# A gated scan followed by a mixture of experts: wo products of each expert's third set and the join of its outputs moved, Gelu of c11 behind the third copy of z, transposes behind the fourth z product

## The chip, the core and the metric

The kernel runs on one core of a Trainium2 chip. The metric is the device time of a run in microseconds, lower is better. A run is one execution of the whole program; the profile is of one execution of its own, taken by the hardware profiler.

Engines are called as the profile calls them: PE (TensorE, matmul; PEld its weight loads), DVE (VectorE), ACT (ScalarE), POOL (GpSimd), SP (SyncE, which issues most of the DMAs).

## The reference, cut to what matters

```python
def reference(x, w_qkva, gamma, router_w, w0, w1, wo):      # x: 8 x 1024 x 256, all float32
    x = x + attn(layernorm(x), w_qkva, gamma)               # rmsnorm, projections, gated scan over the tokens
    return x + ffn(layernorm(x), router_w, w0, w1, wo)

def ffn(x, router_w, w0, w1, wo):                           # 8 groups of 1024 tokens, 8 experts
    logits = einsum('GSM,ME->GSE', x, router_w)
    dispatch, combine = gating_top2(logits, C=256)          # each expert takes up to 256 tokens of a group
    expert_inputs = einsum('GSEC,GSM->EGCM', dispatch, x)
    layer_w0 = einsum('EGCM,EMH->EGCH', expert_inputs, w0)  # M = 256, H = 1368
    layer_w1 = einsum('EGCM,EMH->EGCH', expert_inputs, w1)
    hidden = gelu(layer_w0) * layer_w1
    expert_outputs = einsum('EGCH,EHM->EGCM', hidden, wo)
    return einsum('EGCM,GSEC->GSM', expert_outputs, combine)
```

The change touches only the expert part: the three einsums with w0, w1 and wo.

## The kernel before

**Blocks, experts, sets.** The eight groups are taken in four blocks of two. In each block the eight experts follow each other; an expert has two groups of 256 gathered tokens, and its hidden width of 1368 is cut into six *sets*: five of 256 channels and a last one of 88. There are 4 x 8 x 6 = 192 sets, and `run_set` writes out the instructions of one. This part of the program is scheduled by hand: every engine runs its instructions in the order in which the Python code issues them (`tc.manual_schedule()`).

**The two hidden products with seven matmuls.** For a set, w0 and w1 against the two halves of the model dimension are the 2x2 blocks a11, a12, a21, a22; the tokens of the two groups are the 2x2 blocks b11, b12, b21, b22. Instead of eight block products the kernel uses the seven of a Strassen-Winograd scheme, with sums s1 to s4 of the weights (`row_sums`, on POOL) and t1 to t4 of the tokens (`column_sums`, on DVE). `st.mm` is one such product: one matmul of 128x128 by 256 for each of the set's two chunks of 128 channels. In the trace a float32 matmul leaves two records, so a full-width product shows as four records, all at line L701.

Four products accumulate one after the other in the PSUM bank `z`, and between them ACT copies the running sum out ("snapshots"), because each of them is needed:

- z = a11 b11, copied to `snap0` (L861); the bank `pa` gets a12 b21, and DVE adds both: `c11` (L867), to which ACT applies Gelu (L875 in the kernel before).
- z += s2 t2, copied to `snap1` (L874); the bank `pb` gets s1 t1.
- z += s3 t3, copied to `snap2` (L883); DVE adds it to `pb` and writes half of `hid` (L884).
- z += a22 t4; DVE multiplies z by c11 into the other half of `hid` (L890). The next set starts z anew.
- pb += s4 b22; DVE adds snap1 to it, which is `c12` (L826, `first_sum`). Its Gelu (L829, `first_gate`) and the product with the first half (L833, `second_gate`) are issued in the next set.

So a z product waits for the copy of the one before, and the next set's first z product waits for L890. What is issued on PE between two z products covers the copy.

**The wo products.** `hid` times `wo` of a set is again taken with seven products, with POOL's sums of wo (`out_sums`) and DVE's sums of `hid` (`hid_sums`: L764, then L767 and L768). They are issued two sets later. `out_work` lists them in the order p1, p2, p4, p7, p6, p5, p3 for a full set, or as p2, p3, p4 and x for the set of 88; `products(n)` issues the next n of the list between the z products. Each is one matmul (two records, L753) that accumulates over the six sets of an expert in half of one of four banks: p1 and p6 in y0, p2 and p3 in y1, p7 and p5 in y2, p4 and x in y3. There is one bank of each name, so the next expert's first products must wait until the last expert's sums have been read.

Because of the two sets of delay, an expert's last wo products (those of its sixth set) are issued in the *second* set of the next expert (`st.s == 1`), all four of them ahead of the second z product. In that set `join_outputs` combines the four banks into the output `yT`: part 0 copies half of y0 to `u` on ACT (L798) and adds the rest of y0 and part of y2 on DVE (L799, L800); part 1 adds y1 (L804), y2 (L805) and y3 (L809). The next expert's first wo products, p1 and p2 of its first set, come in its *third* set, behind the first z product.

The last two experts of the last block are `plain`: their wo product is done directly (`outputs`, L733), one set later, in four parts of two matmuls.

**What is put between.** `between()`, called once in a set, puts four 128x128 transposes into the bank `aside`: in the fourth and fifth set of an expert those of the next expert's gathered tokens (`px`, L627, copied by ACT at L630), in the third and sixth those of the last expert's output (`pt_y`, L818, copied by ACT at L717 and then stored by a DMA that SP issues). `pump()`, called twice in a set (behind the pb product in the middle, and at the end), issues the planned pieces of everything else: the scan part of the next block's tokens, its gating, and the sums of the block before. These use the one bank `aside` too.

The lines that the two kernels name alike are a few lines apart: the three copies of z are L861, L874, L883 before and L869, L881, L889 after; L867, L884, L890 and L826 are L875, L891, L898 and L827; Gelu of c11 is L875 before and L890 after. Where the text names a line without more, it is that of the kernel before.

Of the kernel before, what the change touches and what calls it, by code (L numbers as in the profile page):

```python
# [8 lines left out]
FP = mybir.dt.float32  # L9
I32 = mybir.dt.int32  # L10
BF = mybir.dt.bfloat16
AF = mybir.ActivationFunctionType
ALU = mybir.AluOpType
# [4 lines left out]
def kernel(  # L18
# [12 lines left out]
    P = 128  # L31
    B, N, D = x.shape
    NE, _, H = w0.shape
    KC = D // P
    G, S = B, N
    CAP = (int(2.0 * S / NE) + 3) // 4 * 4
# [9 lines left out]
    GB = 2  # L46
# [11 lines left out]
    pb = ctx.enter_context(tc.tile_pool(name="experts", bufs=2))  # L58
# [4 lines left out]
    def bank(tag, name):  # L63
        return psum.tile([P, 512], FP, tag=tag, name=name, bufs=1)
# [600 lines left out]
    def plain(n, e):  # L665
        return n == NB - 1 and e >= NE - 2
# [91 lines left out]
    def hid_sums(st, half):  # L758

        b11, b12, b21, b22 = [st.hid[:, g, k, :] for k in range(2) for g in range(2)]  # L760
        V = nc.vector
        if half == 0:
            st.tw = pb.tile([P, 4, CAP], FP, tag="tw", name=f"tw_{st.n}_{st.e}_{st.s}", bufs=2)
            V.tensor_tensor(st.tw[:, :2, :], st.hid[:, 1], st.hid[:, :, 0], ALU.subtract)  # L764
            return
        t1, t3, t2, t4 = (st.tw[:, i, :] for i in range(4))
        V.tensor_tensor(t2, b22, t1, ALU.subtract)  # L767
        V.tensor_tensor(t4, b21, t2, ALU.subtract)  # L768
        st.t = t1, t2, t3, t4

    def out_work(st):

        if plain(st.n, st.e):
            return [lambda q=q: outputs(st, q) for q in range(4)]
        if st.s == NS - 1:
            def one(name, g, i):
                hs = st.hs
                add_product(st, name, wos[st.j][:hs, 0, i * P : (i + 1) * P], st.hid[:hs, g, 0, :])
            return [lambda: one("p2", 0, 0), lambda: one("p3", 0, 1),
                    lambda: one("p4", 1, 0), lambda: one("x", 1, 1)]  # L780
        a11, a12, a22, s1, s2, s3, s4 = osums.pop(st.j)
        b11, b21, b22 = st.hid[:, 0, 0, :], st.hid[:, 0, 1, :], st.hid[:, 1, 1, :]
        t1, t2, t3, t4 = st.t
        return [lambda p=p: add_product(st, *p) for p in (
            ("p1", a11, b11), ("p2", a12, b21), ("p4", s4, b22), ("p7", s3, t3),
            ("p6", s2, t2), ("p5", s1, t1), ("p3", a22, t4),
        )]

    yts = {}

    def join_outputs(n, e, part):

        V = nc.vector
        acc = {k: ys[n, e, i] for k, (i, half) in ACC.items()}
        halves = [acc[k].rearrange("p (h s) -> p h s", h=2) for k in ("p1", "p2", "p7", "p4")]
        if part == 0:
            u = yts["u"] = pb.tile([P, 3, CAP], FP, tag="u", name=f"u_{n}_{e}", bufs=1)
            nc.scalar.copy(u[:, 0, :], halves[0][:, 0, :])  # L798
            V.tensor_tensor(u[:, 1, :], u[:, 0, :], halves[0][:, 1, :], ALU.add)  # L799
            V.tensor_tensor(u[:, 2, :], u[:, 1, :], halves[2][:, 0, :], ALU.add)  # L800
            return
        u = yts.pop("u")
        yt = pb.tile([P, 2, GB, CAP], FP, tag="yT", name=f"yT_{n}_{e}", bufs=1)
        V.tensor_tensor(yt[:, :, 0, :], u[:, 0::2, :], halves[1], ALU.add)  # L804
        V.tensor_tensor(  # L805
            yt[:, :, 1, :], u[:, 1:3, :],
            halves[2][:, 1:2, :].to_broadcast([P, 2, CAP]), ALU.add,
        )
        V.tensor_tensor(yt[:, :, 1, :], yt[:, :, 1, :], halves[3], ALU.add)  # L809
        for i in range(4):  # L810
            ys.pop((n, e, i))
        yts[n, e] = yt

    def output_rows(n, e, gl):
        pt = ps_a(f"pt_y{n}_{e}_{gl}")
        for hh in range(NH):
            for i in range(2):
                nc.tensor.transpose(  # L818
                    pt[:, hh * D + i * P : hh * D + (i + 1) * P],
                    yts[n, e][:, i, gl, hh * P : (hh + 1) * P], ident,  # L820
                )
        keep_output(n, e, gl, pt)

    def first_sum(st):
        st.c12 = st.ten("cg", "c12", 3)
        nc.vector.tensor_tensor(st.c12, st.snap1, st.cut(st.pb), ALU.add)  # L826

    def first_gate(st):
        nc.scalar.activation(st.c12, st.c12, AF.Gelu_apprx_tanh)  # L829

    def second_gate(st):
        h22 = st.h2[: st.hs, 1, st.wide]
        nc.vector.tensor_tensor(h22, h22, st.c12, ALU.mult)  # L833

    def run_set(j, last, due, pump, between):


        V, A = nc.vector, nc.scalar
        st = Set(j)
        a11, a12, a22, s1, s2, s3, s4 = st.a  # L840
        b11, b21, b22, t1, t2, t3, t4 = st.b
        nm = f"{st.n}_{st.e}_{st.s}"
        z, p_a, p_b = bank("z", f"z_{nm}"), bank("pa", f"pa_{nm}"), bank("pb", f"pb_{nm}")
        st.pb = p_b
        st.hid = pb.tile([P, GB, 2, CAP], FP, tag="hid", name=f"hid_{nm}", bufs=3)
        st.h2 = st.hid.rearrange("p g c s -> p g (c s)")
        zz = st.cut(z)
        work = [f for o in due for f in out_work(o)]
        summed = last and last.s < NS - 1 and not plain(last.n, last.e)
        joined = units[units.index((st.n, st.e)) - 1] if st.s == 1 and j > NS else None  # L850
        if joined and plain(*joined):
            joined = None

        def products(share):
            for _ in range(min(len(work), share)):
                work.pop(0)()

        more = 2 * (len(due) > 1)
        st.mm(z, a11, b11, True)
        snap0 = st.ten("snap", "sn0", 4)  # L860
        A.copy(snap0, zz)  # L861
        if last:
            first_gate(last)
        products(2 + more)
        st.mm(p_a, a12, b21, True)
        c11 = st.ten("cg", "c11", 3)
        V.tensor_tensor(c11, snap0, st.cut(p_a), ALU.add)  # L867
        if last:
            second_gate(last)  # L869
        if st.s == 1:  # L870
            products(2)
        st.mm(z, s2, t2, False)
        st.snap1 = st.ten("snap", "sn1", 4)
        A.copy(st.snap1, zz)  # L874
        A.activation(c11, c11, AF.Gelu_apprx_tanh)  # L875
        products(1 + more)
        if joined:
            join_outputs(*joined, 0)
        st.mm(p_b, s1, t1, True)
        pump()  # L880
        st.mm(z, s3, t3, False)  # L881
        snap2 = st.ten("snap", "sn2", 4)
        A.copy(snap2, zz)  # L883
        V.tensor_tensor(st.h2[: st.hs, 1, st.wide], snap2, st.cut(p_b), ALU.add)  # L884
        if summed:
            hid_sums(last, 0)
        products(2)
        between()
        st.mm(z, a22, t4, False)  # L889
        V.tensor_tensor(st.h2[: st.hs, 0, st.wide], zz, c11, ALU.mult)  # L890
        products(8)  # L891
        st.mm(p_b, s4, b22, False)
        first_sum(st)
        if summed:
            hid_sums(last, 1)
        if joined:
            join_outputs(*joined, 1)
        pump()  # L898
        return st

# [72 lines left out]
    with tc.manual_schedule():  # L973
        last, pending, late = None, [], [[] for _ in range(UB)]
        for n in range(NB):
# [22 lines left out]
            def pump():  # L998
                for f in plan.pop(at[0], []):
                    f()  # L1000
                j, half = at[0] // 2 + n * NE * NS, at[0] % 2
                e, s = at[0] // (2 * NS), j % NS
                nxt = (n, e + 1) if e + 1 < NE else (n + 1, 0)
                if nxt in units:
                    if half == 0 and s == 0 and e + 1 < NE:
                        gather_unit(*nxt)
                    if s == (4, 5)[1 - half]:
                        column_sums(*nxt, 1 - half)
                at[0] += 1

            def between():
                q = at[0] // 2
                e, s = q // NS, q % NS
                nxt = (n, e + 1) if e + 1 < NE else (n + 1, 0)
                if s in (3, 4) and nxt in units:
                    input_channels(*nxt, s - 3)
                before = (n, e - 1) if e > 0 else (n - 1, NE - 1)
                if s in (2, 5) and before in yts:
                    output_rows(*before, s // 5)
                    if s == 5:  # L1020
                        yts.pop(before)

            for j in range(n * NE * NS, (n + 1) * NE * NS):
# [4 lines left out]
                due = [o for o in pending if due_in(o) <= j]  # L1028
                pending = pending[len(due):]
                last = run_set(j, last, due, pump, between)  # L1030
# [41 lines left out]
```

## Time and profile before

| | us |
|---|---|
| median of 3 runs | 2142.76 (2138.98 to 2143.45) |
| the profiled execution, its own time | 2141.66 |
| its span in the profile | 2139.7 |
| first set to the start of the last one | 130.5 to 2111.7 |

The span is cut by the expert sets: they run from 130.5 us to the end, but for some 25 us. Before them come the loads and the first block's scan. In the table of groups a row reads: line, engine, operation, output <- inputs (buffer numbers left out), shape, count; busy time and mean of one; idle time of the engine ahead of such instructions, and what ended it. In the view of waits a row reads: who waited, for whom, in total, how often, the longest. In a timeline a row reads: start, length, engine, line, operation, tiles, count, and in brackets the idle time ahead of it with what ended it. A matmul's end is modelled: in a dense stream the records start closer than they are long.

### The profile page before, as it was taken

Reading aid. Unit: us, or ns where it says so; the run is one execution under the profiler, and the core shown is the slowest. Engines: PE = TensorE matmul, PEld = TensorE weight load, DVE = VectorE, ACT = ScalarE, POOL = GpSimd, SP = SyncE. Lnnn points to the kernel's source line nnn. Section 1 sums busy time; section 2 is a strip of 40 time slices with the busy share of each in tenths; the row PEclk is TensorE's granted clock in tenths of the full one; section 3 lists DMA queues with packets and bytes.
Section 4 is the critical chain, followed back from the end, with each engine's and each line's share of the span. In section 5 each row is a group of like instructions: output and inputs, shape, how many; then the busy total and the mean of one; then the engine's idle time right before and its main releaser. Section 6 shows DMA issues by size and latency. Waiting matters only on the chain.

```text
span 2139.7 us, 27414 instructions
## 1 busy us (share of the span) xinstructions
PE 2002.6 (94%) x9352; PEld 1616.2 (76%) x9352; DVE 1360.3 (64%) x2616; ACT 680.1 (32%) x1286; POOL 1205.9 (56%) x1754
## 2 busy tenths in 40 slices
PE   8899999999999999999999999999899999999958
PEld 4567877777787877777777887787778888878737
DVE  4666666567666575767766666666776666666425
ACT  3333332332333333232323333333333333333211
POOL 3345554555355665656546566666556666666362
PEclk9989999999999999999999999999999999999989
DMA  5223333233233434334323434343433334334251
GB/s 177 80 81 87 99 102 104 82 96 103 73 106 98 121 92 143 112 101 125 111 78 115 123 91 128 102 133 104 119 91 107 114 114 128 119 110 126 83 161 40
DMA packets 224074, 228.83 MB, mean 107 GB/s; under 512 B 32449, under 2 KB 215745, under 8 KB 223937
## 3 DMA queue, kind: packets, MB, share of 16 engines
q1 hardware_dynamic: 211104, 193.51, 30.6%
q0 software_dynamic: 12288, 33.57, 5.3%
q8 instruction: 76, 1.25, 0.2%
q14 instruction: 62, 0.50, 0.1%
q10 hardware_dynamic: 544, 0.01, 0.0%
HBM read 185.61 MB, written 41.42 MB: 106 GB/s over the span
## 4 chain that ended last, share of the span: by engine, by line
PE 81%; DVE 13%; issue 2%; ACT 2%; POOL 1%; another core or an unknown queue 0%; DMA 0%; SPq 0%; ACTq 0%; DVEq 0%; POOLq 0%
PE z L701 26%; PE acc L753 21%; PE pb L701 13%; PE pa L701 7%; PE pa L237 2%; PE pkv L237 2%; PE pq L237 2%; PE py L733 2%; DVE tw L768 1%; DVE c L826 1%; PE px L627 1%; PE pl L303 1%; PE pt_y L818 1%; DVE tw L767 1%; ACT sn L883 1%
## 5 line engine op out<-in xcount | busy, mean ns | idle before, releaser
L657 POOL TENSOR_TENSOR sb<-w 128x256 f32<-128x256 f32 x188 | 133.4, 710 | 543.1 <-PE pb L701 542.0
L701 PE MATMUL z<-tb,sb 128*128 128x256 f32 (+1 forms) x1408 | 369.0, 381 | 0.5 <-ACT sn L874 0.4
L701 PEld LDWEIGHTS z<-tb,sb 128*128 128x128 f32 (+1 forms) x1408 | 258.1, 187 | 55.2 <-issue 14.9
L884 DVE TENSOR_TENSOR hid<-sn,pb 128x512 f32<-128x512 f32 x192 | 122.8, 640 | 267.2 <-ACT sn L883 234.2
L861 ACT COPY sn<-z 128x512 f32<-128x512 f32 x192 | 105.6, 550 | 535.8 <-PE z L701 497.9
L753 PE MATMUL acc<-hid,wo 128*128 128x256 f32 x840 | 223.6, 383 | 27.1 <-DVE yT L804 27.1
L753 PE MATMUL acc<-tw,so 128*128 128x256 f32 x900 | 244.1, 380 | 0.0
L701 PE MATMUL z<-tb,w 128*128 128x256 f32 (+1 forms) x704 | 193.0, 393 | 48.8 <-ACT sn L883 30.1
L867 DVE TENSOR_TENSOR c<-sn,pa 128x512 f32<-128x512 f32 x192 | 122.6, 639 | 156.4 <-PE pa L701 140.9
L874 ACT COPY sn<-z 128x512 f32<-128x512 f32 x192 | 105.5, 550 | 354.5 <-PE z L701 341.3
L826 DVE TENSOR_TENSOR c<-sn,pb 128x512 f32<-128x512 f32 x192 | 123.2, 642 | 141.0 <-PE pb L701 135.6
L753 PEld LDWEIGHTS acc<-hid,wo 128*128 128x128 f32 x840 | 157.6, 190 | 60.2 <-DVE yT L804 38.7
L701 PE MATMUL pb<-xT,sb 128*128 128x256 f32 (+1 forms) x704 | 187.5, 386 | 16.3 <-DVE hid L884 16.2
L701 PE MATMUL z<-xT,w 128*128 128x256 f32 (+1 forms) x704 | 191.0, 390 | 3.1 <-DVE hid L890 2.4
L753 PEld LDWEIGHTS acc<-tw,so 128*128 128x128 f32 x900 | 171.6, 191 | 25.5 <-issue 0.3
L701 PE MATMUL pb<-tb,sb 128*128 128x256 f32 (+1 forms) x704 | 184.2, 380 | 0.0
L701 PE MATMUL pa<-xT,w 128*128 128x256 f32 (+1 forms) x704 | 183.5, 379 | 0.6 <-ACT hT L190 0.6
L701 PEld LDWEIGHTS z<-tb,w 128*128 128x128 f32 (+1 forms) x704 | 118.0, 188 | 82.4 <-ACT sn L883 52.4
L701 PEld LDWEIGHTS z<-xT,w 128*128 128x128 f32 (+1 forms) x704 | 127.0, 190 | 48.5 <-DVE hid L890 18.1
L883 ACT COPY sn<-z 128x512 f32<-128x512 f32 x192 | 105.3, 548 | 182.3 <-PE z L701 158.5
L701 PEld LDWEIGHTS pb<-xT,sb 128*128 128x128 f32 (+1 forms) x704 | 131.0, 189 | 42.3 <-DVE hid L884 14.3
L659 POOL TENSOR_TENSOR sb<-w 128x256 f32<-128x256 f32 x188 | 150.9, 802 | 0.0
(176 smaller groups left out, 3740.7 us busy)
## 6 DMA issues: line engine op xcount, KB each, us to landing
w<-in_L_ffn_w_kernel_dram SPq DMA_DIRECT2D x320, 256.0 KB
wo<-in_L_ffn_wo_kernel_dram SPq DMA_DIRECT2D x160, 256.0 KB
y<-ot SPq DMA_DIRECT2D x62, 256.0 KB
xt<-in_L_attn_x_dram SPq DMA_DIRECT2D x16, 512.0 KB
x<-xt SPq DMA_DIRECT2D x16, 512.0 KB
xn<-xn SPq DMA_DIRECT2D x16, 512.0 KB
xc<-x SPq DMA_DIRECT2D x16, 512.0 KB
out_dram<-xc SPq DMA_DIRECT2D x12, 512.0 KB
```

The costliest lines, as they stand in the source:

```text
L237: nc.tensor.matmul(pp, lhsT=wT[:, k, c * P : (c + 1) * P], rhs=t["hT"][:, k, :], start=(k == 0), stop=(k == KC - 1),)
L657: eng.tensor_tensor(s1, a21, a22, ALU.add)
L659: eng.tensor_tensor(s3, a11, a21, ALU.subtract)
L701: nc.tensor.matmul(ps[:hs, i * CAP : (i + 1) * CAP], lhsT=a[:, i * hs : (i + 1) * hs], rhs=b, start=first and i == 0, stop=True, skip_grou ...
L733: nc.tensor.matmul(po[:, hh * D : (hh + 1) * D], lhsT=st.hid[:hs, gl, i, hh * P : (hh + 1) * P], rhs=wos[st.j][:hs, i, :], start=(s == 0 a ...
L753: nc.tensor.matmul(ys[n, e, i][:, half * CAP : (half + 1) * CAP], lhsT=lhsT, rhs=rhs, start=fresh, stop=True, skip_group_check=True,)
L826: nc.vector.tensor_tensor(st.c12, st.snap1, st.cut(st.pb), ALU.add)
L861: A.copy(snap0, zz)
L867: V.tensor_tensor(c11, snap0, st.cut(p_a), ALU.add)
L874: A.copy(st.snap1, zz)
L883: A.copy(snap2, zz)
L884: V.tensor_tensor(st.h2[: st.hs, 1, st.wide], snap2, st.cut(p_b), ALU.add)
```

## The change

It moves work within a set; the arithmetic is the same.

- p1, p2 and p4 of an expert's first set all come behind the second z product of its third set (before: p1 and p2 behind the first, p4 behind the second).
- `join_outputs` has three parts: part 0 as before; part 1 (the addition of y1, L804) behind the third copy's sum; part 2 (y2 and y3) behind `first_sum`. In that set `hid_sums(last, 0)` goes to the end.
- Gelu of c11 is issued behind the third copy of z instead of the second.
- `between()` is called behind the fourth z product instead of ahead of it.
- The plain experts' parts are spread one by one.

```diff
@@ join_outputs
-        u = yts.pop("u")
-        yt = pb.tile([P, 2, GB, CAP], FP, tag="yT", name=f"yT_{n}_{e}", bufs=1)
-        V.tensor_tensor(yt[:, :, 0, :], u[:, 0::2, :], halves[1], ALU.add)
+        if part == 1:
+            yt = yts[n, e] = pb.tile([P, 2, GB, CAP], FP, tag="yT", name=f"yT_{n}_{e}", bufs=1)
+            V.tensor_tensor(yt[:, :, 0, :], yts["u"][:, 0::2, :], halves[1], ALU.add)
+            return
+        u, yt = yts.pop("u"), yts[n, e]
...
@@ run_set
-        def products(share):
-            for _ in range(min(len(work), share)):
+        if st.s == 1:
+            shares = [2, 2, 0, 0, 0]
+        elif len(due) > 1:
+            shares = [1, 1, 2, 2, 2]
+        elif due and plain(due[0].n, due[0].e):
+            shares = [1, 0, 1, 1, 1]
+        else:
+            shares = [0, 0, 3, 2, 2] if st.s == 2 else [2, 0, 1, 2, 2]
+
+        def products():
+            for _ in range(min(len(work), shares.pop(0))):
                 work.pop(0)()
 
-        more = 2 * (len(due) > 1)
         st.mm(z, a11, b11, True)
...
-        products(2 + more)
+        products()
         st.mm(p_a, a12, b21, True)
...
-        if st.s == 1:
-            products(2)
+        products()
         st.mm(z, s2, t2, False)
         st.snap1 = st.ten("snap", "sn1", 4)
         A.copy(st.snap1, zz)
-        A.activation(c11, c11, AF.Gelu_apprx_tanh)
-        products(1 + more)
         if joined:
             join_outputs(*joined, 0)
+        products()
         st.mm(p_b, s1, t1, True)
         pump()
         st.mm(z, s3, t3, False)
         snap2 = st.ten("snap", "sn2", 4)
         A.copy(snap2, zz)
+        A.activation(c11, c11, AF.Gelu_apprx_tanh)
         V.tensor_tensor(st.h2[: st.hs, 1, st.wide], snap2, st.cut(p_b), ALU.add)
-        if summed:
+        if joined:
+            join_outputs(*joined, 1)
+        elif summed:
             hid_sums(last, 0)
-        products(2)
-        between()
+        products()
         st.mm(z, a22, t4, False)
         V.tensor_tensor(st.h2[: st.hs, 0, st.wide], zz, c11, ALU.mult)
-        products(8)
+        between()
+        products()
         st.mm(p_b, s4, b22, False)
         first_sum(st)
+        if joined:
+            join_outputs(*joined, 2)
+            hid_sums(last, 0)
         if summed:
             hid_sums(last, 1)
-        if joined:
-            join_outputs(*joined, 1)
```

More of the change, by code (lines that the diff above doesn't have):

```diff
@@ L811, in join_outputs @@
             ys.pop((n, e, i))
-        yts[n, e] = yt
     def output_rows(n, e, gl):
```

## The prediction

> **What bounds the kernel now.** I read the page's busy shares first, then the waits over the whole run, then the timeline of one expert's second and third set, engine by engine.
>
> ```profile
> PE 2002.6 (94%) x9352; PEld 1616.2 (76%) x9352; DVE 1360.3 (64%) x2616; ACT 680.1 (32%) x1286; POOL 1205.9 (56%) x1754
> PE 81%; DVE 13%; issue 2%; ACT 2%; POOL 1%; another core or an unknown queue 0%; DMA 0%; SPq 0%; ACTq 0%; DVEq 0%; POOLq 0%
> ```
>
> TensorE is busy 94% and carries 81% of the chain that ended last. The order change adds no matmul and no transpose, so it can act only on the 137 us in which PE is idle (2139.7 - 2002.6). These waits of PE (and what feeds them) are what the change can touch:
>
> ```profile
> ACT c L875 <- DVE c L867: 45.7, 34, 3.7
> PE z L701 <- ACT sn L883: 30.1, 39, 2.2
> PE acc L753 <- DVE yT L804: 27.1, 28, 1.4
> PE pb L701 <- DVE hid L884: 16.2, 13, 1.9
> PE py L733 <- DVE hid L833: 9.9, 9, 4.6
> ```
>
> The third row is the target: 28 stalls for about 30 experts. One of them, PE alone:
>
> ```profile
> 1705.93 1.13 PE L701 MATMUL z<-tb,w 128*128 128x256 f32 x4 [0.73 <-ACT sn L883]
> 1706.90 1.03 PE L701 MATMUL pb<-xT,sb 128*128 128x256 f32 x4
> 1707.86 1.13 PE L701 MATMUL z<-xT,w 128*128 128x256 f32 x4
> 1708.82 0.59 PE L753 MATMUL acc<-hid,wo 128*128 128x256 f32 x2
> 1710.54 0.70 PE L753 MATMUL acc<-hid,wo 128*128 128x256 f32 x2 [1.12 <-DVE yT L804]
> 1711.08 1.03 PE L701 MATMUL pa<-xT,w 128*128 128x256 f32 x4
> ```
>
> Back-to-back records start 0.216 us apart (pb at 1717.99, next z at 1718.85, four records), though each shows 0.38 us; so four records are 0.86 us. The two products of the third set (p1, p2) should take 1708.82 to 1709.68, and pa starts at 1711.08: 1.40 us lost, of which 1.12 is shown as idle. p2 accumulates into bank y1, and the join's L804, which reads y1, comes last on VectorE, behind first_sum (L826) and two hid sums (L767, L768). The chain view also has a stall of 18.20 us ("issue") at 2068 and one of 9.71 at 2056, while POOL issues 32 indirect loads back to back; this is not the work that is reordered.
>
> **What the skill says.** "Perfetto Trace Analysis", Optimization Strategy: look for gaps on the engine that should be saturated and make what releases them start sooner; repeated equal bubbles can mean too few buffers. The trace agrees: 28 gaps averaging 0.97 us, all released by one instruction, on accumulators with one bank each. "PSUM — Partial Sum Buffer", Engine vs sequencer instructions: the queues of ScalarE and VectorE are strictly first in, first out. The trace agrees: Gelu of c11 (L875) waits 3.62 us at 1514.44 for L867, and the third copy L883, whose input was ready, runs only behind it, at 1514.76.
>
> **The change, part by part.** The built orders of SyncE (every DMA) and GpSimd are the same in both kernels; only PE, VectorE and ScalarE differ. Durations are of the profiled execution (span 2139.7, its own time 2141.66), which lies 1.1 us under the median 2142.76; I make the sum against 2141.66.
>
> (1) p1 and p2 of each third set go from behind the first z product to behind the second, just ahead of p4; L804 goes from the end of the second set to behind its L884. Then L804 ends some 4 us before p1 is issued instead of after it, and L805 and L809 (0.68 each) directly follow first_sum and are done some 2.3 us after the second set's PE end, while p4 now comes 3.4 us after it (z, pa, z, p1, p2). The stall goes. Size: 27.1 us shown, plus per stall the 0.17 hidden under the shown end (0.38 - 0.216) and the slow following record (0.32 instead of 0.216): 29 x 0.27 = 7.8. **-35 us**; bounds: 27 to 40.
>
> (2) What p1 and p2 covered. In the third set only pa (0.86) now lies between the first z product and the second, which waits for the first copy. That copy starts 0.20 after z's issue ends, takes 0.59, and PE follows 0.05 after a copy (1705.29 + 0.59, PE at 1705.93): 0.84 against 0.86. No stall, unless ScalarE is busy. Its queue ahead of that copy is free: the moved Gelu ran in the set before. **0**; bounds 0 to +5.
>
> (3) The transposes (four px or pt_y, 0.44 us together) leave the gap between the third and fourth z products in sets 3 to 6; two products (0.86) stay. L883's copy starts 0.255 after z3 and ends at 0.84, with 0.05 following: 0.89. So 0.03 of stall x 3 full-width sets x 31 = **+3 us**; bounds 0 to +6. Sets 1 already run so (no transposes there). The sixth set's narrow copy (0.36) is covered. Each step takes along ScalarE's evacuation (L717 or L630, 0.59) and, for pt_y, the y store; 0.86 us later. The bank "aside" is needed again only after two products and pb (1.7 us); the store's readers are in the next block. Two pt_y stalls on "DVE xt L276" (5.6 us together) are put off by one product: **-1**, bounds 0 to -3.
>
> (4) Gelu of c11 goes behind the third copy. The copy no longer waits for c11. In the second set, z4 has no product before it in either kernel, so its 0.73 us (31 x 0.73 = 22.6 of the 30.1) stays. The rest is mostly first and sixth sets in which VectorE is behind: at 1515.16 PE waits 2.16. But L884 is queued on VectorE behind L833, L645 and L646, ending at 1516.12, and the last pb needs it: it would start at 1516.2 rather than 1516.5. So of some 7 us I take **-1.5**. Does the later Gelu delay L890, which frees z for the next set? The copy ends at 0.84, Gelu (0.63) at 1.5 after z3; z4 ends at 1.72 to 1.75. L890 waits for z4 anyway. Cost 0; the cover is 0.25 us of ScalarE being free.
>
> (5) In the second set the join's copy u (L798) stood behind that Gelu (0.63) and L799 waits for it (49.8 us over 30). It now runs 0.5 to 0.63 earlier, so the token work and L884 behind it do too. Of PE's 16.2 us on L884 about half is in second sets with such work: **-4**; bounds 0 to -7. L804 takes the place of L764 (0.67 against 0.69) ahead of L890: nothing changes there.
>
> (6) Last block's plain experts: from two, one, one outputs to one each behind four of the z products; the third output, which needs L833, moves two slots later. Waits of 9.9, of which 4.6 lies in the unexplained stall at 2056: **-5**; bounds 0 to -8. One extra L764 (0.69 us on VectorE, once) is hidden.
>
> (7) Give-back. VectorE still has 4.0 us at the seam (L826, L805, L809, L764, L767, L768) ahead of the third set's c11, and PE now arrives 1.1 to 1.4 us sooner. L884 of the third set must end before the last pb, 8.6 us after that set's start; VectorE without token work ends it at 7.2, with the 3.6 us of BN statistics and a top-2 step at 8.6 to 9.5. Some 6 to 10 of the experts are like that: **+5**; bounds 0 to +20.
>
> Sum: -35 + 3 - 1 - 1.5 - 4 - 5 + 5 = -38.5; 2141.66 - 38.5 = **2103 us**.
>
> **Rivals.** *VectorE takes the place of the stall.* For: 64% busy, and in every third set its queue is continuous from L826 to L867. Against: the stall's own releaser L804 is moved out of that queue's tail, and L884 has 1.4 us to spare in plain sets. If it holds for every expert at 0.9 us, 28 us come back: about 2131.
> *Better than the forecast.* The lower ends of (5), (6) and of the pt_y part come true, (4) brings its whole 7 us, and nothing is given back: -35 + 3 - 3 - 7 - 7 - 8 = -57, about 2085.
> *Slower: the late Gelu becomes the release of z.* Place: L890 of every set waits for c11, then frees z for the next set's first product. From 0.25 us of ScalarE delay between the third copy and Gelu, L890 moves; from some 1.1 us (0.25 and its present slack of 0.83: L890 ends at 1718.02, z starts at 1718.85) PE waits. If Gelu is that late by 0.3 us more in all 191 sets, PE loses 57 us and the kernel ends near 2160 (2103 + 57). Against it: in the trace nothing else stands on ScalarE between those two, and it is 32% busy.
> *It doesn't do what it says* is excluded for the order (the built order has it); but the stall at 2056 to 2087 could shift by some 10 us either way.
>
> **Chances.** Forecast 60%, VectorE rival 18%, better 12%, slower 7%, about no change 3% (within 0.2%, 4.3 us, about what a measurement of this kernel can tell from none). The range from 2085 to 2130 takes in the bounds of (1) and (7), most of the rival and the better case, and leaves out the slower case and the tails. Faster 0.90, same 0.03, slower 0.07.
>
> **What would show it.** The row PE acc <- DVE yT disappears; no new row of PE z <- first copy above 5 us; PE z <- third copy stays near 23 to 30; L799's wait falls from 49.8 to about 30; PE pb <- hid (the L884 of now) between 10 and 30. Above 40 there, or a row PE z <- DVE hid (L890) above 20, the forecast is wrong in (7) or (4). PE busy stays near 2002 and the idle falls from 137 to about 100.

## The result and the profile after

The changed kernel takes 2113.59 us (median of 4 runs, 2110.05 to 2116.74) against 2142.75 before: a ratio of 0.9867 [0.9848, 0.9886], 29 us less. The forecast was 2103. Of the profiled executions, after took 2110.05 and before 2141.66, 31.6 less; the terms of the forecast are compared with these two traces.

The busy shares and the chain of the kernel after, from its page:

```profile
PE 2007.9 (95%) x9352; PEld 1609.5 (76%) x9352; DVE 1370.5 (65%) x2617; ACT 681.8 (32%) x1286; POOL 1223.4 (58%) x1754
PE 85%; DVE 9%; issue 2%; ACT 2%; POOL 1%; DMA 0%; another core or an unknown queue 0%; SPq 0%; ACTq 0%; DVEq 0%; POOLq 0%
```

Same matmuls, span 2108.2, so PE is idle 100.3 us instead of 137.1. But its busy time grew by 5.3 us for the same 9352 records; in the table of groups the fourth z products (full width) grew from 172.9 to 181.7 us, 393 to 407 ns each. Their rows, before and after:

```profile
L701 PE MATMUL z<-tb,w 128*128 128x256 f32 x640 | 172.9, 393 | 44.0 <-ACT sn L883 25.3 <-issue 18.5
L701 PE MATMUL z<-tb,w 128*128 128x256 f32 x640 | 181.7, 407 | 40.7 <-ACT sn L889 23.9 <-issue 16.7
```

That is the first hint of what went wrong: records that are longer though nothing was added. From the view of waits of the kernel after, the rows that matter here:

```profile
PEld z L701 <- ACT sn L889: 69.4, 152, 1.1
DVE u L799 <- ACT u L798: 34.9, 30, 1.3
PE z L701 <- ACT sn L889: 23.9, 33, 0.7
PE pb L701 <- DVE hid L891: 21.1, 17, 3.0
PE z L701 <- issue: 16.7, 2, 16.0
ACT c L890 <- DVE c L875: 10.7, 8, 2.3
PE pt_y L819 <- DVE xt L276: 4.7, 2, 2.4
PE py L733 <- DVE hid L834: 2.1, 2, 1.5
```

The row of PE acc <- DVE yT is gone. Gelu's wait for c11 fell from 45.7 to 10.7 us, since Gelu is asked for later; the join's L799 waits 34.9 instead of 49.8. PE's wait for the third copy is 23.9 (30.1 before) and looks as forecast. The first row doesn't: the *weight loads* of the fourth z product now wait for that copy 152 times; before they did so 65 times:

```profile
PEld z L701 <- ACT sn L883: 52.4, 65, 2.4
```

A third set of the kernel after (1689.95 to 1699.83), PE alone, cut to the places that are read here:

```profile
1689.95 1.13 PE L701 MATMUL z<-xT,w 128*128 128x256 f32 x4
1690.91 1.03 PE L701 MATMUL pa<-xT,w 128*128 128x256 f32 x4
1691.85 1.10 PE L701 MATMUL z<-tb,sb 128*128 128x256 f32 x4
1692.78 1.03 PE L753 MATMUL acc<-hid,wo 128*128 128x256 f32 x4
...
1695.81 1.03 PE L753 MATMUL acc<-tw,so 128*128 128x256 f32 x4
1696.70 1.13 PE L701 MATMUL z<-tb,w 128*128 128x256 f32 x4
1697.67 0.60 PE L819 MATMUL pt_y<-ident,yT 128*128 128x128 f32 x4
...
1699.83 0.38 PE L701 MATMUL z<-xT,w 128*128 128x256 f32 x1
```

From its first z product to the next set's it takes 9.88 us; the like set before took 10.99 (1707.86 to 1718.85). The 1.4 us in front of the third set's first acc products is gone. But two smaller losses came, which have no idle bracket. The second z product (1691.85) starts 0.94 behind pa, not 0.86, and the product behind it another 0.93 later: 0.15 lost. The fourth z product (1696.70) starts 0.89 behind acc, and the transposes 0.97 behind it: 0.14 lost. The four-record rows show it in their length: 1.10 and 1.13 instead of 1.03.

Why a copy that comes 0.03 us late costs 0.13 shows in another set of the kernel after, where the fourth z product has two products ahead of it (timeline, all engines):

```profile
1676.78 0.84 PEld L753 LDWEIGHTS acc<-tw,so 128*128 128x128 f32 x4
1676.99 1.03 PE L753 MATMUL acc<-tw,so 128*128 128x256 f32 x4
1677.25 0.59 ACT L889 COPY sn<-z 128x512 f32<-128x512 f32 x1 [1.57 <-PE z L701]
...
1677.88 0.73 PEld L701 LDWEIGHTS z<-tb,w 128*128 128x128 f32 x4 [0.27 <-ACT sn L889]
1677.88 1.13 PE L701 MATMUL z<-tb,w 128*128 128x256 f32 x4
```

In the dense stream a load starts 0.21 us ahead of its matmul (1676.78 and 1676.99). The fourth z product's load waits for the copy too, and the copy ends at 1677.84. So load and matmul start together at 1677.88: the product is 0.03 late, and its first record takes 0.32 instead of 0.216, 0.104 more. The next record in the stream (acc, at 1678.85) comes 0.97 behind z instead of 0.86. The Trainium skill ("TensorE: Matmul & The Clock Gate", Step-by-step: what each phase is for) says that TensorE pulls weight loads ahead of matmuls in flight, so that the next tile's weights load while this one's matmul runs. The trace agrees for the dense stream (0.21 us ahead) and shows that the lead is lost where the matmul's wait comes late.

How much lead is needed can be read from the first records of the full-width products of the kernel after. With a lead under 0.02 us (204 products, 159 of them fourth z products) the first record takes 0.32 us, with 0.03 us (69 products) 0.29, with 0.11 us (174 products, nearly all behind transposes) 0.218, and with the 0.21 of the dense stream 0.216. So about 0.1 us of lead is enough. The copy lets the load start 0.89 us behind the end of the third z product's issue; to lose nothing, the cover has to last some 0.1 longer, about 1.0 us (an estimate from these figures: no run has a cover between 0.86 and 1.30). Two products give 0.86; three give 1.30; two and the four transposes, as before, also 1.30.

The second z product of the third set is a little different. In the set above the first copy ends at 1691.70, but the load starts only at 1691.81 and the matmul at 1691.85, and so in all 30 of these sets: 0.11 from the copy's end to the load instead of 0.05, with a semaphore instruction of PE between them. The matmul is 0.07 late and its first record takes 0.29, 0.07 more: 0.14.

The following sums are from the starts of all PE records in both traces, as excess over the dense pitch (0.216 us a record of 128x256, 0.109 a transpose). By length of the sets, after less before: first sets +1.8, second -4.1, third -26.3, fourth +5.3, fifth +3.7, sixth -3.1, all sets with a plain expert's work -8.1, outside the sets -0.6; together -31.4 us.

| stall, us | before | after |
|---|---|---|
| third sets, first acc products | 35.2 | 0 |
| third sets, second z product | 0 | 4.3 |
| fourth z product, third, fourth and fifth sets | 0.7 | 9.6 |
| fourth z product, first sets | 6.2 | 4.0 |
| fourth z product, second sets | 30.9 | 30.9 |
| last pb, second sets | 9.3 | 4.7 |
| last pb, first and third sets | 6.0 | 9.7 |
| sixth sets: pt_y / fourth z / last pb | 9.0 / 6.1 / 6.5 | 5.8 / 0 / 12.7 |

### The profile page after: what moved, and what is told of

Same layout as the page of the kernel before. It is cut to its first block, busy times and chain, and to the rows that moved or that the text cites. A ratio compares the mean times of both kernels' runs of the same rounds, so it can differ in the third digit from the quotient of the medians.

```text
span 2108.2 us, 27798 instructions
## 1 busy us (share of the span) xinstructions
PE 2007.9 (95%) x9352; PEld 1609.5 (76%) x9352; DVE 1370.5 (65%) x2617; ACT 681.8 (32%) x1286; POOL 1223.4 (58%) x1754
## 4 chain that ended last, share of the span: by engine, by line
PE 85%; DVE 9%; issue 2%; ACT 2%; POOL 1%; DMA 0%; another core or an unknown queue 0%; SPq 0%; ACTq 0%; DVEq 0%; POOLq 0%
PE z L701 29%; PE acc L753 21%; PE pb L701 14%; PE pa L701 7%; PE pa L237 2%; PE pkv L237 2%; PE pq L237 2%; PE py L733 2%; PE px L627 1%; PE pl L303 1%; PE pt_y L819 1%; ACT sn L889 1%; PE po L270 1%; DVE hid L834 1%; PE pc L591 1%
## 5 line engine op out<-in xcount | busy, mean ns | idle before, releaser
L657 POOL TENSOR_TENSOR sb<-w 128x256 f32<-128x256 f32 x188 | 133.0, 708 | 504.9 <-PE pb L701 501.4
L891 DVE TENSOR_TENSOR hid<-sn,pb 128x512 f32<-128x512 f32 x192 | 122.6, 639 | 244.0 <-ACT sn L889 206.6
L701 PE MATMUL z<-tb,w 128*128 128x256 f32 (+1 forms) x704 | 200.8, 404 | 40.7 <-ACT sn L889 23.9
L753 PE MATMUL acc<-hid,wo 128*128 128x256 f32 x840 | 216.2, 380 | 0.0
L701 PE MATMUL pb<-xT,sb 128*128 128x256 f32 (+1 forms) x704 | 187.2, 385 | 21.1 <-DVE hid L891 21.1
L753 PEld LDWEIGHTS acc<-tw,so 128*128 128x128 f32 x900 | 162.3, 191 | 18.2
L701 PEld LDWEIGHTS pb<-xT,sb 128*128 128x128 f32 (+1 forms) x704 | 130.8, 189 | 47.7 <-DVE hid L891 23.9
L660 POOL TENSOR_TENSOR sb<-w,sb 128x256 f32<-128x256 f32 x188 | 157.5, 838 | 0.0
```

The lines of the kernel that those rows point to most:

```text
L657: eng.tensor_tensor(s1, a21, a22, ALU.add)
L660: eng.tensor_tensor(s4, a12, s2, ALU.subtract)
L701: nc.tensor.matmul(ps[:hs, i * CAP : (i + 1) * CAP], lhsT=a[:, i * hs : (i + 1) * hs], rhs=b, start=first and i == 0, stop=True, skip_grou ...
L753: nc.tensor.matmul(ys[n, e, i][:, half * CAP : (half + 1) * CAP], lhsT=lhsT, rhs=rhs, start=fresh, stop=True, skip_group_check=True,)
```

## The experiments

The **theory** after seeing this: the join's move works in full; the transposes' move costs some 9 us, because two products don't cover the copy and the load's lead with it; p1 and p2 taken from the third set's second z product cost 4. The **rivals**: VectorE gives the missing time back; or the transposes cost because of where they went, with their evacuations on ScalarE, and not because cover was taken away.

The first four kernels were compared with before on one chip (here *the quick chip*), where before took 2117.53 us; the next four on another (*the slow chip*), where it took 2142.84, as in the first runs. What differs between the chips is told at the end. The changed kernel was run on the slow chip only. Where a run of the quick chip is set against it here, its 29 us of gain are taken to hold there too. Both ratios are known to some 3 us each way, so such a difference is good to some 4 us, and each is held against the stalls in its trace as well.

### The join alone

The kernel before with the join in three parts and p1, p2, p4 behind the second z product; Gelu, transposes and plain experts as before:

```diff
-        products(2 + more)
+        third = st.s == 2 and len(due) == 1 and not plain(due[0].n, due[0].e)
+        products(0 if third else 2 + more)
...
-        products(1 + more)
+        products(3 if third else 1 + more)
```

> The kernel before with part (1) of the change alone: the join in three parts, hid_sums moved with it, and p1, p2, p4 of the third set behind the second z product; Gelu, the transposes and the plain experts' shares stay as before. Theory (each wait costs by its cover; a z product whose copy is covered by only two matmuls also loses the weight load that should run ahead, about 0.14 us each): the 35 us of stall behind L804 go, 4.3 us come back at the third set's second z product, so 2142.75 - 31 = 2112, about as fast as the whole change, because the other parts of the change cancel each other (transposes +9, Gelu and u copy -5, plain experts -8, VectorE give-back +3). Rival (the missing 10 us are VectorE's backlog behind the join): this part alone carries the backlog, so it gains only 35 - 14 = 21 us, 2122, and the third set shows a row PE pb <- DVE hid of 10 us or more.

Measured: 2093.52 us, ratio 0.9885 [0.987, 0.99], 24 less than before. In the trace the acc stall is 0 (35.2 before), but the third set's second z product costs 4.1, its last pb 3.8 (1.8), its transposes of pt_y 2.4 (0) and its fourth z product 1.0 (0.1); first sets are 2.4 longer. So the stall went whole, and besides the 4.1 some 8 us come back, which the theory's figure had left out: its 31 was too much, and the 24 lies nearer to the rival's 21. The rival's sign, 10 us or more at the last pb of third sets, did not come. VectorE is the releaser at the last pb and in part at pt_y; what makes the first sets longer was not tried.

### Transposes back ahead of the fourth z product

The kernel after, one line put back:

```diff
         products()
+        between()
         st.mm(z, a22, t4, False)
         V.tensor_tensor(st.h2[: st.hs, 0, st.wide], zz, c11, ALU.mult)
-        between()
```

> The changed kernel with the transposes put back ahead of the fourth z product. Theory: the fourth z product of sets 3, 4 and 5 then has 1.30 us of cover again in place of 0.86, its 0.135 us each (9.0 us in the trace of after) vanish: 2113.6 - 9 = 2105. Rival (the transposes' move pays, by giving VectorE time to read z before the next set): slower than the changed kernel, 2117 or more, with new waits of the first z product on VectorE.

Measured: 2078.15 us, ratio 0.9818 [0.9804, 0.9831], 39 less than before, some 10 better than the whole change (by set lengths of the two traces, 8). The stalls of the fourth z product in the third, fourth and fifth sets are 0.1, 0.0 and 0.0 again, and fourth and fifth sets are within 1.4 us of before. Its waits:

```profile
PEld z L701 <- ACT sn L889: 47.3, 68, 1.1
PE z L701 <- ACT sn L889: 24.6, 34, 0.7
```

The weight loads wait 68 times, not 152. PE's own row hardly moved (23.9 to 24.6): it counts only idle time beyond the shown end of a record, and these losses were below that.

### Gelu back behind the second copy

```diff
         A.copy(st.snap1, zz)
+        A.activation(c11, c11, AF.Gelu_apprx_tanh)
...
         A.copy(snap2, zz)
-        A.activation(c11, c11, AF.Gelu_apprx_tanh)
```

> The changed kernel with Gelu of c11 put back behind the second copy of z. Theory: in second sets the join's copy u stands behind Gelu again, L799 waits about 50 us in total instead of 35, the last pb of second sets waits 4 us more, and first and sixth sets wait for the third copy again (+3): 2113.6 + 6 = 2120. Rival (Gelu's place is worth nothing, all gain is the join's): within 2 us of the changed kernel.

Measured: 2096.05 us, ratio 0.9897 [0.9882, 0.9912], 21.5 less than before; with Gelu moved the kernel is some 7 us better. Its waits:

```profile
DVE u L799 <- ACT u L798: 49.9, 30, 2.1
PE z L701 <- ACT sn L890: 42.3, 52, 2.6
PE pb L701 <- DVE hid L891: 16.7, 12, 2.5
```

L799 waits 49.9 again, as in the kernel before: it is this move that brings 15 us there. And it shows a give-back: in the sixth sets the fourth z product loses 16.5 and the last pb 6.1 here, against 0 and 12.7 with Gelu moved. Of 16.5 us, 6.6 are taken back one product later, at VectorE's L891. By set lengths, Gelu's move is worth 3.9 us in second sets, 3.2 in third and 2.8 in sixth sets, and costs 2.1 in first sets.

### p1 back behind the first z product of the third set

```diff
-            shares = [0, 0, 3, 2, 2] if st.s == 2 else [2, 0, 1, 2, 2]
+            shares = [1, 0, 2, 2, 2] if st.s == 2 else [2, 0, 1, 2, 2]
```

> The changed kernel with p1 alone put back behind the third set's first z product (p2 and p4 stay behind the second). Bank y0, into which p1 accumulates, is read last by L799 in the middle of the second set, so p1 need not wait. Theory: the second z product's copy is covered by 1.30 us, and the 0.14 us at it (4.3 us in the trace of after) vanish: 2113.6 - 4 = 2109. Rival (p1 waits for the join as p2 did, because the whole join is what releases the banks): +20 us or more, 2134.

Measured: 2084.01 us, ratio 0.9841 [0.9827, 0.9854], 33.5 less than before. That is some 4 better than the whole change, no more than such a difference is good to. In the trace the second z product of the third set loses 0 instead of 4.3, and third sets are 3.9 us shorter; but first sets are 4.1 longer, nearly all of it in three experts. So it is shown that the local loss goes, and not that the whole kernel gains by it. The rival, 20 us slower, is excluded. p1 goes into bank y0, which L798 and L799 read early in the join, so it can return without bringing the old stall back; of the two, only p2 goes into y1.

### The changed kernel again, and three products as cover

The changed kernel on the slow chip, for comparison (the expectation below calls this chip the first, and the quick one the second):

> The changed kernel itself, once more, on the chip of the next three runs, so that they are compared with it directly. In the runs so far the stall of 16 to 18 us in the last block's plain set (2068 us in the kernel before) was in both traces of the first chip and in none of the second, where the kernel before took 2117.5 us. Every theory expects the same gain as before, 29 us in 2117.5 or in 2142.8, because the stall is in both kernels or in neither.

Measured: 2113.42 us, ratio 0.9867 [0.9852, 0.9882]: the same as in the first runs.

With the transposes left behind the fourth z product, three products instead of two ahead of it; this separates the cover from the place:

```diff
-            shares = [0, 0, 3, 2, 2] if st.s == 2 else [2, 0, 1, 2, 2]
+            shares = [0, 0, 3, 3, 1] if st.s == 2 else [2, 0, 1, 3, 1]
```

> The changed kernel with three wo products ahead of the fourth z product instead of two, in first, third, fourth, fifth and sixth sets; the transposes stay behind it. Theory (cover alone decides): 1.30 us of cover again, the 0.135 us at the fourth z product vanish in sets 3 to 5 and in first sets too (9 + 3 us): about 11 us under the changed kernel. Rival (it was the transposes' place, not the cover, that made the 10 us of the run with the transposes put back): within 3 us of the changed kernel.

Measured: 2100.2 us, ratio 0.98 [0.9783, 0.9817], 13 under the changed kernel (single runs from 2094.61 to 2103.99). The rival of the place falls: the transposes and their evacuations still stand behind the fourth z product, and its stalls are 0 in third to fifth sets (9.6 before this edit) and in the first (4.0). The same set as in the timeline above, in this kernel:

```profile
1669.19 1.27 PEld L753 LDWEIGHTS acc<-tw,so 128*128 128x128 f32 x6
1669.40 1.46 PE L753 MATMUL acc<-tw,so 128*128 128x256 f32 x6
1669.66 0.59 ACT L889 COPY sn<-z 128x512 f32<-128x512 f32 x1 [1.57 <-PE z L701]
...
1670.49 0.84 PEld L701 LDWEIGHTS z<-tb,w 128*128 128x128 f32 x4
1670.70 1.03 PE L701 MATMUL z<-tb,w 128*128 128x256 f32 x4
```

The copy ends at 1670.25, ahead of the load's turn. The load leads by 0.21 again and the four records take 1.03.

### Products into the gap of the second set

Both kernels have no product ahead of the fourth z product of the second set, and lose 0.9 us and the lead there, 0.73 of it shown as idle. Two of its four products are put there:

```diff
-            shares = [2, 2, 0, 0, 0]
+            shares = [2, 0, 0, 2, 0]
```

> The changed kernel with the second set's four products split: p2 and p3 behind the first z product, p4 and x ahead of the fourth (before and after the change all four came ahead of the second). Theory: the largest wait left, the 0.9 to 1.0 us at each second set's fourth z product (30.9 us), falls to about 0.135 each, -26 us; but VectorE frees z at the same time as before (L898 behind L891 and L804), so the next set's first z product waits 0.3 to 0.4 more in the sets without work in between: +8. Together about 18 us under the changed kernel. Rival (VectorE is the bound at this seam): the whole wait moves to the last pb and the next z, within 5 us of the changed kernel.

Measured: 2088.52 us, ratio 0.9743 [0.973, 0.9756], 25 under the changed kernel where 18 were expected. The gain of 26 came, or nearly (29.9 to 4.8 at the fourth z product). The loss of 8 at the next set's first z product did not (5.7 in both): the fourth z product starts where it started before, 0.89 behind the end of the third's issue, only the gap is filled, so L898 behind it is no later. PE's wait for the third copy, in the changed kernel's run on this chip and then here:

```profile
PE z L701 <- ACT sn L889: 35.6, 34, 11.8
PE z L701 <- ACT sn L889: 6.3, 4, 4.4
```

Of the 35.6, 11.8 is one stall, the chip's, which in this run falls on other rows; the count, 34 to 4, is the edit's. The join's L799 waits only 9.5 in this run.

### All of it together

Three products ahead of each fourth z product wherever there are that many, p1 back, one product left behind the first z product of the second set, and the join's L804 moved behind L898's multiply (it reads bank y1, into which p3 now comes later):

```diff
-            shares = [2, 2, 0, 0, 0]
+            shares = [1, 0, 0, 3, 0] if joined else [2, 2, 0, 0, 0]
...
-            shares = [0, 0, 3, 2, 2] if st.s == 2 else [2, 0, 1, 2, 2]
+            shares = [1, 0, 2, 3, 1] if st.s == 2 else [2, 0, 1, 3, 1]
...
-        if joined:
-            join_outputs(*joined, 1)
-        elif summed:
+        if summed and not joined:
             hid_sums(last, 0)
...
         V.tensor_tensor(st.h2[: st.hs, 0, st.wide], zz, c11, ALU.mult)
+        if joined:
+            join_outputs(*joined, 1)
         between()
```

> All that the runs point to: three wo products ahead of the fourth z product in every full set (in second sets p3, p4 and x), p1 back behind the third set's first z product, and the join's L804 behind L898 instead of ahead of it. Theory: 11 (as the run with three products) + 4 (p1) + 30 (second set) = 45 us under the changed kernel, less about 8 that VectorE takes back. Rival (VectorE's seam): 25 us or less under the changed kernel, with PE pb <- DVE hid above 40 us.

Measured: 2065.14 us, ratio 0.964 [0.9626, 0.9653], 48 under the changed kernel, where 37 to 45 were expected, and 78 under the kernel before. The rival, 25 us or less with the row of the last pb above 40, is excluded. Busy shares of its page, and then its waits:

```profile
PE 1982.7 (96%) x9352; PEld 1624.9 (79%) x9352; DVE 1370.8 (66%) x2617; ACT 681.8 (33%) x1286; POOL 1218.2 (59%) x1754
```

```profile
PEld z L701 <- ACT sn L889: 23.6, 8, 19.4
PE pb L701 <- DVE hid L891: 21.1, 15, 3.7
PE z L701 <- ACT sn L889: 20.6, 4, 18.6
```

The weight loads wait for the third copy 8 times instead of 152. Of the 20.6 us, 18.6 are one stall, which is the chip's and is told at the end. PE's busy time is 25.2 us less than in the kernel after with the same 9352 records, 15.5 of it in the full-width fourth z products (181.7 to 166.2): their long first records are gone. The gains of the three parts measured apart (13, 4 and 25) make 42. Of the other 6, some 4 lie at the second sets' fourth z product (4.8 in the run above, 1.1 here), which has three products ahead of it here instead of two; the rest is within the error, and the join's new place and the product left behind the first z product were not run apart. Beside the one stall, the largest row of PE that is left is its wait for VectorE at the last pb: 21.1 here, and between 16 and 22 us in the kernel before and in all of the changed ones.

## Why the prediction was right, and where its sizes were off

The direction, the mechanism of the main gain and the range held. The profiled execution lies 7 us above the forecast's 2103, the median 11. That it came so close is in part luck, as the terms show:

1. **The acc stall, -35:** 35.2 to 0. Right, including what was added for the time hidden under the shown end of a record.
2. **The third set's second z product, 0 (0 to +5):** +4.3. Mis-sized. The step compared 0.84 with 0.86 and found the copy in time for the matmul. Its 0.05 between the copy's end and PE was taken from the fourth z product; here it is 0.11 to the load and 0.14 to the matmul, which makes the matmul 0.07 late, and with the lead lost the first record adds 0.07. Putting p1 back removed it.
3. **The transposes, +3 (0 to +6):** +8.9, from 0.7 to 9.6 in the table. This is the step that failed, and outside its own bounds. "0.03 of stall" was right (1677.88 instead of 1677.85). What was left out is the 0.104 of the slow first record behind it: 0.03 + 0.104 = 0.134 a set. The very same record, 0.32 instead of 0.216, had been counted in step 1 and forgotten here. The bounds of the step were drawn about the 0.03 alone. The small gain at pt_y came (its waits on xt fell from 5.6 to 4.7, all stalls in front of these transposes in sixth sets from 9.0 to 5.8).
4. **Gelu of c11, -1.5 of some 7:** in the sixth sets 6.1 less at the fourth z product and 6.2 more at the last pb, so nothing there; in first sets 2.2 less and 2.1 more. The argument that VectorE's L891 takes it back is what the traces show. The run with Gelu put back shows more that the term left out: in the changed kernel, with less cover at the fourth z product, Gelu's move is also worth 3.2 us in third and 2.8 in sixth sets. PE's wait for the multiply that frees z grew only from 2.4 to 4.6 us, so the cost of 0 for the later release nearly held, and the slower rival, which needs 57, fell.
5. **The join's copy u earlier, -4:** second sets -4.1, their last pb from 9.3 to 4.7. Right; L799's wait fell to 34.9, not quite to 30.
6. **Plain experts, -5 (0 to -8):** -8.1, of which 2.4 lie in the set with the unexplained stall and have nothing to do with the step. At the edge of the bound; L834's wait went from 9.9 to 2.1.
7. **Give-back by VectorE, +5 (0 to +20):** PE's wait for L891 rose by 4.9 (16.2 to 21.1), which looks like the 5, but this is a coincidence. In third sets, where the step placed it, the last pb rose by 1.6 only (1.8 to 3.4). Second sets fell by the 4.6 of term 5, first sets rose by 2.1 and sixth sets by 6.2; with Gelu alone put back those two are at 4.2 and 6.1 again, as before (4.2 and 6.5), so they are the price of term 4. The rival that made it the whole stall again is excluded by the third sets, which kept 26.3 us.

Steps 2 and 3 together cost 13.2 instead of 3, and step 6 gave 3 more than forecast: a net loss of 7 against the forecast, the distance between 2103 and the profiled 2110.05; what the other terms were off, a few us each way, happens to cancel. The checks named beforehand (PE's idle at about 100, the row of the third copy between 23 and 30) came out as written, but for L799's wait at 34.9 instead of 30; none of them looked at the weight loads or at the length of records, so none could show this error. The forecast that PE's busy time stays near 2002 was the one that did not hold exactly (2007.9), and it was the right place to look.

## What to carry to other kernels

When work between two dependent matmul groups is taken away, compare the cover with the moment at which the releaser lets the weight load start, plus the lead that the load needs (here about 0.1 us), not with the matmul's start: a release 0.03 us late cost 0.134, and one wo product more of cover (0.86 to 1.30) was worth some 13 us in the run that changed nothing else. Read the weight loads' row in the waits and the mean length of the records beside the idle column of the matmuls, which hides losses of this size. Then look for gaps with no work in them at all: two products moved into the second set's gap brought 25 us, nearly as much as the whole change.

## What the hardware showed that was not expected

**The lead of the weight load.** In float32, with 128x256 matmuls, a product whose load could not run ahead has a first record of 0.32 us instead of 0.216 (204 products in the kernel after). A lead of 0.03 us gives 0.29, and 0.11 us already gives 0.218: half of the dense stream's lead of 0.21 is enough.

**A stall that differs between the chips.** In the plain sets of the last block, where POOL issues 32 indirect loads back to back, PE, ScalarE and VectorE stand still for a while. PE's row gives no releaser:

```profile
2086.64 2.08 PE L701 MATMUL z<-tb,w 128*128 128x256 f32 x4 [18.20 <-issue]
```

(before), and the one of after:

```profile
2056.04 2.08 PE L701 MATMUL z<-tb,w 128*128 128x256 f32 x4 [15.98 <-issue]
```

But it is not PE that stops first. The third copy of z, for which PE waits there, starts as late (before):

```profile
2086.01 0.59 ACT L883 COPY sn<-z 128x512 f32<-128x512 f32 x1 [19.24 <-remote]
```

It ends at 2086.60 and PE goes on 0.04 behind it. "remote" is another core or a queue that the profile does not know. The other traces of the slow chip show the same: a copy on ACT or an addition or multiply on DVE starts late, and PE follows it. Where the stall falls differs from kernel to kernel.

On the quick chip it is absent in all four traces: there the third sets with plain work take 24 us together, and 50 in the trace of before on the slow chip; the kernel before takes 2117.53 us instead of 2142.84, which is 25 less. What holds ScalarE and VectorE there was not tried and stays open; that the indirect loads do is only argued from their being there.
